# Linear attention with a router gate on one core: one operand split issued a step later, and twelve result stores issued after two more loads

## The chip, the core and the metric

The kernel runs on one core of a Trainium2 chip. The core has five engines that work side by side, each through its own queue in order: TensorE (PE) multiplies matrices, VectorE (DVE), ScalarE (ACT) and GpSimd (POOL) work element by element, and SyncE (SP) issues most of the DMA transfers here. Weight loads of TensorE are shown as a row of their own (PEld); a DMA queue's issuing is shown as SPq. The metric is the time of one execution on the device in microseconds (us), as the median of several runs. A profiled execution is recorded once, and its span is counted from the first to the last recorded event.

## The reference

Four sequences of 512 tokens with 512 features are worked on. All of it is float32.

```python
xn = layernorm(x)                                     # x: (4, 512, 512)
qkv = silu(xn @ w_qkv.T)                              # 16 heads of 128: q, k, v
for each block of 64 tokens, per head:                # kv: running 128x128 state
    o  = (q * q_decay) @ kv + ((q @ k.T) * diag_decay) @ v
    kv = block_decay * kv + (k * k_decay).T @ v
o = norm_w * (o * rsqrt(mean(o * o) + 1e-6))          # mean over all 2048 channels
s = (sigmoid(xn @ w_gate.T) * o) @ w_out.T
scores = softmax(xn @ router_w.T + router_b)          # 64 experts
w8, i8 = top_k(scores, 8)
g = silu(xn * sum(w8) + w8 @ expert_bias[i8])
out = x + s * g
```

## The kernel before, in words

The token blocks of the attention are 128 wide instead of 64 (four chunks, NT = 4, per sequence), which computes the same. The big products keep float32 accuracy with three passes: an operand is split into a high part in a rounded type (split_hi, a copy on ScalarE, L100) and a low part (split_lo, a subtraction on VectorE or GpSimd, L103), and high by high, high by low and low by high are added in PSUM. The projections of two sequences at a time use a scheme with seven products in place of eight (unit, L484).

The work comes in three stages. The first computes v for all sequences and keeps it in DRAM. The second goes through head units: for two pairs of sequences and for each pair of heads one gate unit and two q/k units (L1039 to L1095). A unit issues its seven products, and after each of them the entries of a list, after[0] to after[6], in which other work is placed: the attention of the head before, loads, splits of coming weights. The attention of a head is written in three parts: scores_qk (products sa of k and q, transposes kt of k, the mask product at on VectorE, kd on ScalarE, qd on GpSimd), states (ss, and its running sums st) and attend (o, the product y with gate and norm weight on VectorE, a store of y to DRAM, and a square on ScalarE that GpSimd adds up in sqs). When a q or k comes out of a unit, its silu is done in two parts: the sigmoid is issued at once on ScalarE (L555), and the product on VectorE (L558) is put into a list, deferred, which do_deferred empties later.

The third stage is the output projection, a loop over 64 steps (L1112), one for each sequence and head. A step multiplies the split output weight of its head (wr) with the split y of its head and sequence (yr) into four PSUM banks pos, twelve products in all (o_head, L816). A function, ahead(i, loads, splits) at L1015, issues what the steps need before: loads of y (and of the output weight wo for the first sequence) up to step i + loads, and their splits up to step i + splits. One split step consists of a copy on ScalarE and a subtraction on VectorE for yr, and, for the first sequence, a copy on ScalarE and a subtraction on GpSimd for wr. From step 2 on the pool op2 has four buffers each of yin, woin and yr, so that a load waits until the split of four steps before has read its buffer.

The last head unit issues the first calls of ahead in its lists. After the unit comes do_deferred at L1109, which issues the product of the last k. The attention of the last head is issued in the first three steps of the loop, behind their twelve products each: scores_qk in step 0, states in step 1, attend in step 2 (L1100 to L1104). Its PSUM tiles, those of sa, kt and ss and one of the o, take turns in the three buffers of ps_sc; the products pos are in ps_mm.

After the sixteenth head of a sequence, finish (L808) is called for each of its four token tiles: VectorE scales the bank by the norm and by the gate u (L811), GpSimd (VectorE for the last sequence) adds x (L812), and the result is stored (L813). Behind these come in program order ahead of that step, then the next sequence's first step, which loads wT, the turned routing weights of the next sequence, and the first tile of x (L1149 to L1151). Four steps into a sequence ffn (L764) multiplies wT with the expert biases into pu and begins the next gate u, out of a pool with five buffers; silu_gate (L772) completes it.

All orders on the queues are those of the program text; nothing is reordered by a planner.

## Time and profile before

| | us |
|---|---|
| median of 3 runs | 1069.27 |
| lowest and highest run | 1067.15 and 1069.29 |
| profiled execution | 1068.67 |
| its span | 1066.9 |
| TensorE busy in the span | 1056.2 |
| VectorE, ScalarE, GpSimd busy | 695.6, 476.1, 727.3 |
| last head unit's products end, step 0 of the output projection begins | about 865.7 |
| step 16 (second sequence) begins | about 924.8 |

The mean granted clock of TensorE over the span is 0.997 of full speed. A row of a timeline gives start, length, engine, line, operation, what is written and read, and in brackets how long the engine had been idle and what released it. A row of the chain of work that ended last gives start, length and what the chain was on. Busy TensorE is modelled, since its matmuls are pipelined.

### The profile page before, as it was taken

The page shows a single profiled execution, that of the slowest core. Times are in us where ns is not written, and L with a number is a line of the kernel's source. Part 1 is how long each engine was busy: PE and PEld are TensorE (multiplying, and loading weights), DVE is VectorE, ACT ScalarE, POOL GpSimd, SP SyncE. Part 2 cuts the span into 40 slices and gives each one's busy share as a digit, 9 for nine tenths or more (in the row PEclk, how much of TensorE's full clock was granted, in tenths as well). Part 3 has the DMA queues.
Part 4 walks back from the last instruction along what each step waited for, and adds up shares of the span by engine and source line. Part 5 has one row for each costly group of instructions (what it writes and reads, how often), then busy time and mean ns, then how long its engine had stood idle before and what let it go on. Part 6 is the DMA issues. An engine that isn't in the chain of part 4 may idle for free.

```text
span 1066.9 us, 16491 instructions
## 1 busy us (share of the span) xinstructions
PE 1056.2 (99%) x5771; PEld 910.9 (85%) x5771; DVE 695.6 (65%) x1061; ACT 476.1 (45%) x923; POOL 727.3 (68%) x710
## 2 busy tenths in 40 slices
PE   9999999999999999999999999999999989999998
PEld 8888788888888888888888888888888878888886
DVE  7898876667576666665756756657567556754464
ACT  5555554544444444444444444444444434332321
POOL 5898892868787678777785787777867847612130
PEclk9999999999999999999999999999999999999999
DMA  6557747522423333235722232232222436354351
GB/s 224 184 177 251 262 145 235 160 84 88 136 84 94 103 97 108 75 124 195 254 84 83 87 115 78 85 128 84 84 91 90 149 109 206 119 178 168 98 194 53
DMA packets 109875, 143.11 MB, mean 134 GB/s; under 512 B 9680, under 2 KB 58208, under 8 KB 108896
## 3 DMA queue, kind: packets, MB, share of 16 engines
q1 hardware_dynamic: 108752, 141.35, 40.7%
q8 instruction: 46, 0.75, 0.3%
q10 hardware_dynamic: 1040, 0.71, 0.2%
q14 instruction: 37, 0.30, 0.1%
HBM read 93.24 MB, written 50.87 MB: 135 GB/s over the span
## 4 chain that ended last, share of the span: by engine, by line
PE 93%; DVE 3%; DMA 2%; POOL 1%; SPq 1%; issue 1%; ACT 1%; DVEq 0%; ACTq 0%
PE u_qk L502 28%; PE po L818 16%; PE u_g L502 14%; PE u_v L502 11%; PE sa L675 5%; PE o L712 5%; PE ss L698 4%; PE o L714 4%; PE kt L678 2%; DMA raw_v<-in_w_v_dram 1%; PE lg L318 1%; PE pu L769 1%; DMA v<-vo_v 1%; DVE k L558 1%; POOL ts L268 0%
## 5 line engine op out<-in xcount | busy, mean ns | idle before, releaser
L818 PE MATMUL po<-wr,yr 128*128 128x512 f32 (+1 forms) x777 | 179.5, 389 | 1.0 <-DVE u L811 1.0
L818 PEld LDWEIGHTS po<-wr,yr 128*128 128x128 f32 x777 | 144.5, 188 | 31.2 <-DVE u L811 1.2
L502 PE MATMUL u_qk<-blk_T,ws_qk 128*128 128x512 f32 x576 | 147.1, 395 | 0.0
L724 POOL TENSOR_TENSOR sqs<-sqs,sq 128x512 f32<-128x512 f32 x60 | 78.5, 1309 | 78.3 <-ACT sq L723 78.3
L502 PEld LDWEIGHTS u_qk<-blk_T,ws_qk 128*128 128x128 f32 x576 | 105.7, 188 | 20.5
L103 DVE TENSOR_TENSOR yr<-yin,yr 128x512 fp32r<-128x512 f32 x64 | 71.5, 1127 | 50.1 <-ACT yr L100 50.0
L103 POOL TENSOR_TENSOR ws_qk<-sum_qk,ws_qk 128x512 fp32r<-128x512 f32 x64 | 82.8, 1295 | 30.7 <-ACT ws_qk L100 29.9
L502 PE MATMUL u_qk<-blk_B,wa_qk 128*128 128x512 f32 x384 | 99.1, 393 | 0.0
L558 DVE TENSOR_TENSOR k<-k,sg_k 128x512 f32<-128x512 f32 x64 | 92.3, 1442 | 2.4 <-ACT sg_k L555 2.2
L712 PE MATMUL o<-at,vin 128*128 128x128 f32 x512 | 88.4, 275 | 0.0
L502 PEld LDWEIGHTS u_qk<-blk_B,wa_qk 128*128 128x128 f32 x384 | 70.9, 188 | 14.2
L702 DVE SCALAR_TENSOR_TENSOR st<-st,bdecay,ss 128x128 f32<-128x128 f32 x128 | 41.7, 346 | 61.4 <-ACT st L700 59.1
L555 ACT ACTIVATE sg_k<-k 128x512 f32<-128x512 f32 x64 | 40.5, 632 | 86.6 <-DVE k L493 86.6
L712 PEld LDWEIGHTS o<-at,vin 128*128 128x128 f32 x512 | 74.9, 191 | 2.5
L502 PE MATMUL u_g<-blk_T,ws_g 128*128 128x512 f32 x288 | 76.0, 399 | 0.0
L714 PE MATMUL o<-qd,st 128*128 128x128 f32 x384 | 74.2, 275 | 0.0
L103 POOL TENSOR_TENSOR ws_g<-sum_g,ws_g 128x512 fp32r<-128x512 f32 x32 | 42.7, 1334 | 44.7 <-ACT ws_g L100 44.7
L675 PE MATMUL sa<-q,k 128*128 128x128 f32 x512 | 68.7, 278 | 3.2 <-DVE k L558 3.2
L675 PEld LDWEIGHTS sa<-q,k 128*128 128x128 f32 x512 | 65.1, 193 | 6.6 <-issue 3.2
L777 POOL TENSOR_TENSOR u<-u,sgu 128x512 f32<-128x512 f32 x16 | 20.7, 1292 | 70.1 <-ACT sgu L776 57.4
L716 DVE SCALAR_TENSOR_TENSOR y<-o,nw,gt 128x512 f32<-128x512 f32 x64 | 47.6, 747 | 31.7 <-PE o L714 30.1
L723 ACT ACTIVATE sq<-o 128x512 f32<-128x512 f32 x60 | 35.9, 598 | 71.4 <-POOL sqs L724 43.1
(186 smaller groups left out, 2420.5 us busy)
## 6 DMA issues: line engine op xcount, KB each, us to landing
v<-vo_v SPq DMA_DIRECT2D x64, 256.0 KB, 2.1
raw_qk<-in_w_head_dram SPq DMA_DIRECT2D x64, 256.0 KB, 3.6
vin<-v SPq DMA_DIRECT2D x64, 256.0 KB, 3.6
y<-y SPq DMA_DIRECT2D x64, 256.0 KB, 2.0
yin<-y SPq DMA_DIRECT2D x64, 256.0 KB, 3.0
x<-in_x_dram SPq DMA_DIRECT2D x32, 256.0 KB, 4.3
raw_g<-in_w_head_dram SPq DMA_DIRECT2D x32, 256.0 KB, 3.2
raw_v<-in_w_v_dram SPq DMA_DIRECT2D x16, 256.0 KB, 5.6
```

Of the source, the lines that this page charges most:

```text
L103: eng.tensor_tensor(lo, src, hi.bitcast(F32), ALU.subtract)
L502: nc.tensor.matmul(ps, lhsT, rhs, start=(first and c == 0 and n == 0), stop=(c == KC - 1 and n == len(PASSES) - 1), skip_group_check=not f ...
L555: nc.scalar.activation(sg, src, AF.Sigmoid)
L558: nc.vector.tensor_tensor(dst, src, sg, ALU.mult)
L675: nc.tensor.matmul(pa[:, c], k[:, c], q[:, c], start=True, stop=True)
L698: nc.tensor.matmul(ps[:, c], kd[s][:, c], v_of(b, h, c), start=True, stop=True)
L702: nc.vector.scalar_tensor_tensor(r[:, c], r[:, c - 1], bdecay[:, h : h + 1], ps[:, c], ALU.mult, ALU.add)
L712: nc.tensor.matmul(o, v_of(b, h, c), at[s][:, c], start=True, stop=(c == 0))
L714: nc.tensor.matmul(o, st[s][:, c - 1], qd[s][:, c - 1], start=False, stop=True)
L716: nc.vector.scalar_tensor_tensor(y, po, nw[:, h : h + 1], gts[s], ALU.mult, ALU.mult)
L724: nc.gpsimd.tensor_tensor(sq[b], sq[b], s1, ALU.add)
L818: nc.tensor.matmul(pos[t][:, c], yr[:, yi, bass.ts(t, P)], wos[h][:, wi, c], start=(h == 0 and n == 0), stop=(h in stops and n == len(PASS ...
```

## The change

Two edits are made. The call of ahead in after[6] of the last head unit asks for two split steps in place of three, so that the split of step 2 (h = 2 of the first sequence) is issued by the call of ahead at the top of step 0, behind do_deferred at L1109. The number of loads that the call asks for is the same. In finish the store of a result is put into a list, stores, for the first three sequences; the list is emptied in the next step of the loop, behind its call of ahead. The four stores of each of the three sequences thus stand behind the y loads that are issued by ahead in the last step of the sequence and in the first step of the next. The stores of the last sequence are issued at once as before.

```diff
+    stores = []
+
     def finish(b, t, ps, c=slice(None)):
         u, xt = gates[b, t][:, c], xts[b, t][:, c]
         last = b == B - 1
         nc.vector.scalar_tensor_tensor(u, ps[:, c], rms[b][:, t : t + 1], u, ALU.mult, ALU.mult)
         (nc.vector if last else nc.gpsimd).tensor_tensor(u, u, xt, ALU.add)
-        (nc.scalar if last and t % 2 else nc.sync).dma_start(out=out[tok(b, t), c], in_=u)
+
+        def store():
+            (nc.scalar if last and t % 2 else nc.sync).dma_start(out=out[tok(b, t), c], in_=u)
+        if last:
+            store()
+        else:
+            stores.append(store)
...
             after[3].append(more)
             after[4].append(lambda: ahead(0, 4, 2))
             after[5].append(lambda: load_eb(op))
-            after[6].append(lambda: ahead(0, 6, 3))
+            after[6].append(lambda: ahead(0, 6, 2))
...
         if h < NH - 1:
             ahead(i, 6, 3)
+            while stores:
+                stores.pop(0)()
         if h == 0:
             for t in range(NT):
                 pos[t] = ps_mm.tile([P, F], F32, tag="mm", name=f"po_{b}_{t}")
```

## The prediction

> **What bounds the kernel now.** First the page's busy rows and its chain by line. TensorE is busy 99% of the span and 93% of the chain is its own work, so only its idle time, and the time in which its clock is not full, can be won.

> ```profile
> PE 1056.2 (99%) x5771; PEld 910.9 (85%) x5771; DVE 695.6 (65%) x1061; ACT 476.1 (45%) x923; POOL 727.3 (68%) x710
> PE 93%; DVE 3%; DMA 2%; POOL 1%; SPq 1%; issue 1%; ACT 1%; DVEq 0%; ACTq 0%
> ```

> An average over 1067 us hides a hole, so next the chain in order of time where the change sits, from the end of the last head unit:

> ```profile
> 869.19 0.52 ACT yr L100
> 869.71 0.02 issue
> 869.73 0.04 DVE yr L103
> 869.77 1.25 issue
> 871.01 1.76 DVE k L558
> 872.77 0.14 issue
> 872.91 2.04 PE sa L675 x8
> 874.95 0.64 PE kt L678 x3
> 875.59 3.15 PE po L818 x12
> ```

> VectorE starts the subtraction of the third y split (yr, L103) at 869.73, and only behind it, at 871.01, the product that completes the last k (L558). ScalarE had the sigmoid for that product long before:

> ```profile
> 865.39 0.63 ACT L555 ACTIVATE sg_k<-k 128x512 f32<-128x512 f32 x1 [1.06 <-DVE k L493]
> 872.91 2.04 PE L675 MATMUL sa<-q,k 128*128 128x128 f32 x8 [2.96 <-DVE k L558]
> ```

> The sigmoid ends at 866.02, the last y of the unit (L716) leaves VectorE at 867.21, and VectorE then sits idle 2.52 us in front of a subtraction that waits for ScalarE's copy, while the ready product stands behind it. TensorE idles 2.96 us for that product. Third, the windows of one us (columns: window, length, busy time of PE, PEld, DVE, ACT, POOL, the granted TensorE clock, DMA share, GB/s):

> ```profile
> 871.00:872.00 1.00, 0.00 (x0) 0.00 (x0) 1.00 (x2) 0.00 (x0) 1.00 (x1) 1.00 0.97 344
> 873.00:874.00 1.00, 1.00 (x5) 1.00 (x6) 0.36 (x1) 0.00 (x0) 1.00 (x2) 0.50 0.78 242
> 876.00:877.00 1.00, 1.00 (x6) 0.76 (x5) 0.25 (x1) 1.00 (x3) 0.00 (x0) 0.87 0.00 0
> ...
> 1060.00:1062.00 2.00, 1.03 (x8) 0.83 (x8) 1.93 (x4) 0.00 (x0) 0.00 (x0) 1.00 0.35 131
> 1062.00:1064.00 2.00, 1.01 (x9) 0.80 (x7) 0.98 (x3) 0.00 (x0) 0.00 (x0) 1.00 0.55 197
> ```

> The idle time also costs clock: 0.50 from 873 until a little after 876. From 876 to 1059 TensorE has no gap but two small ones in front of pu, below.

> **Part 1, the third split moved to step 0.** It consists of two ScalarE copies, one VectorE subtraction (yr) and one GpSimd subtraction (wr). No loads move: the call in the last unit still issues loads 4 and 5, and step 0 finds nothing more to load. On ScalarE and GpSimd the neighbours in the queue stay the same, because between the old and the new place only the deferred product is issued, and that is VectorE's. So the edit is one swap on VectorE: product k first, yr subtraction second. Recomputed in order:

> - Product k starts at 867.2. Alone on VectorE this form takes 0.68 us, beside GpSimd up to 1.75 (the four k products of 840 to 880: 1.17 to 1.75). It ends between 867.9 and 868.95, before TensorE is through with the other sequence's sa and kt at 869.95. The second sa, whose PSUM buffer is freed by ScalarE's square at 869.19, follows without a wait and takes 0.9, as the first did at full clock: until 870.85.
> - The yr subtraction keeps its start, 869.73, and its 1.36: until 871.09. The mask product at (L680) of the first sequence is queued behind it, 0.68 more: until about 871.75. This is late next. ps_sc has three buffers, and by their turns the second kt takes the one that this at reads. So TensorE stands from 870.85 to about 871.9 (0.14 of issue, as at 872.77), a new wait of **1.0 us** in place of 2.96.
> - kt 0.33 and the 12 products of step 1, 2.74 (as step 2's at 880.08), at full clock: step 1 ends at 875.0. Before it ended at 878.74. Gain **3.7 us**: 1.96 of idle time, and 1.7 of slow clock and of waking up (2.04 + 0.64 + 3.15 against 0.9 + 0.33 + 2.74 is 1.86, of which 0.14 is lost again in issue).

> [...] Product k would be issued at 867.2, just ahead of GpSimd's square sum at 867.27. [...] The rows show VectorE stretched more often (1.36 for yr beside GpSimd, 0.68 alone), but GpSimd too (wr 1.72 at 870.49 against 1.27). I take the middle, **3.5 us**.

> [...] The nearest rows are the last two windows above: TensorE busy half the time over 4 us, with one gap of 0.97, and the clock stays 1.00. I take no drop. With a drop, some 3.2 us (what it lasted here) at half speed lose 1.6, and the gain is 1.9. Bounds of this part: 1.9, and 4.6 if no gap stays (the second kt in another buffer).

> Does the shift last? yr of step 2 is ready at 871.1 and its wr at 872.2 (unchanged), step 2 would start near 876.4: 4 us of cover. Steps 5 and 6 are tight: GpSimd's wr for step 5 runs 889.21 to 890.96 and TensorE is there at 891.45; step 6 waits 0.3. But these subtractions stand in GpSimd's queue behind the square sums of the last attention (885.93 to 889.25), which follow TensorE's o matmuls, and the loads of that stage stand in SP's queue behind the y stores of the same attention (885.20). All of it moves with TensorE. The loads for steps 4 and 5 are issued at 867.6 to 869.5 and the DMA engines are idle by 875. The shift goes through.

> **Part 2, twelve stores later.** At the end of the first three sequences SP's queue is:

> ```profile
> 911.18 9.89 SPq L785 DMA_DIRECT2D yin<-y  x4
> 926.11 4.98 SPq L813 DMA_DIRECT2D out_dram<-u  x4
> 931.19 0.87 SPq L785 DMA_DIRECT2D yin<-y  x2
> 932.11 0.42 SPq L761 DMA_DIRECT2D wTin<-wTd  x1
> 936.11 0.30 PEld L769 LDWEIGHTS pu<-ebs,wTin 128*128 128x128 f32 x2 [0.37 <-DMA wTin<-wTd]
> ```

> After the change the two y loads stand ahead of the stores. The first (y of step 20) has its buffer at 924.0, the second when the yr subtraction of step 17 ends at 928.2 (first of three from 926.60). The stores that wait behind it catch up at 0.45 each; the last is bound by GpSimd's add at 930.7 either way, and nothing of VectorE, ScalarE or GpSimd waits for a store soon (the pool has five u). The y loads come 3 to 7 us earlier, which hides in slack already there (yr of step 20 is ready at 935.4, wanted at 936.85). What reaches TensorE: wT is issued at 931.15 in place of 932.11, and pu waits 0.37 for it here and 0.28 at 981.60; the third time it does not wait. Pu took 0.68 and 0.60 there against 0.45 elsewhere: gain 0.23 + 0.15, **0.35 us**. Bounds: 0.4 gained, and 0.4 lost if stores and wT collide in the DMA engines.

> **Sum.** 3.5 + 0.35 = 3.85 us. The profiled execution took 1068.67 with a span of 1066.9: it would be 1064.8 with a span of 1063.05. The median of the runs lies 0.6 above it (1069.27), and two of three runs agree on that value, so the forecast is 1069.27 - 3.85 = **1065.4 us**, 0.36% less. About 0.2% (2.1 us, also the spread of the three runs) is what a measurement can tell from no change.

> **Rivals.**
> - The clock drops in the gap that stays. [...] Against: the two windows at the end. Gain 1.9 + 0.35: 1067.0, on the border of what can be told. 10%.
> - The gain is given back in steps 5 to 7, with GpSimd's wr as the bound. For it: the 0.3 wait and GpSimd's unbroken run from 889 to 899. Against: that run starts from TensorE's own attention. Then only part 2 is left: 1068.9. 11%.
> - Slower: the second y load blocks SP. All four stores, wT and the x loads stand behind it, and pu has no slack for wT at two of three boundaries. It decides once wT slips by more than 1.9 us against before at all three: 3 x 1.9 = 5.7 eats 3.5 and adds the 2.1 that can be seen. With 2.3 us of SP issue between the y load and wT, the yr subtraction would have to end at 931.7 and not at 928.2. Then 1071.5 or more. 7%.
> - No gap stays: 4.6 + 0.35, 1064.3. 6%.
> - My forecast: 66%, own range 1064.4 to 1066.3.

> **How the numbers follow.** The forecast and the case without a gap lie on the faster side, 72%, and half of the clock case, 5%; from this I take 3 for the scatter of the runs: 74% faster. Within 0.2% are half of the clock case, the given-back case and that scatter: 19%. Slower 7%. For eight in ten the range goes from 1063.7 (no gap, less scatter) to 1067.8: forecast and clock case are in, the other two rivals out.

> **What would show it.** Right: in the chain near 867, L558 of k ahead of yr L103; no wait of sa for k; a wait of kt of 1 to 1.5 us for at L680; the clock 1.00 in every us from 868 to 878; step 1 ending near 875; pu at about 932.5 and 978 without a wait for wTin; on SP two loads before the four stores. Wrong: 0.5 clock after 872, a wait of po for wr or yr in steps 4 to 7, a longer wait of pu for wTin, or the same wait of sa for k.

## The result, and the profile after

Over ten runs the changed kernel takes 1064.78 us in the median (1063.93 to 1067.52), and the kernel before, over ten runs that now include the three shown above, 1067.78 (1067.10 to 1069.29). The ratio is 0.9967 with a 95% interval of 0.9956 to 0.9978: 3.5 us faster, 2.4 to 4.7 (3.0 by the two medians). The forecast was 3.85 less, 1065.4. The profiled execution took 1063.93 with a span of 1062.2.

The page of the changed kernel, its busy row and chain by engine:

```profile
PE 1053.3 (99%) x5771; PEld 909.4 (86%) x5771; DVE 696.0 (66%) x1061; ACT 476.3 (45%) x923; POOL 728.7 (69%) x710
PE 87%; DVE 1%; issue 0%; ACT 0%; POOL 0%; DVEq 0%; ACTq 0%
```

TensorE's busy time fell by 2.9 us although it does the same matmuls: a matmul at half clock counts at its full length (the eight sa took 2.04 us at a clock of 0.50 in the kernel before, 0.89 at 1.00 in the chain of split_behind below), so slow ones that are gone show here (1.65 of the 2.9, as the interval below shows). The change is best read in the chain of the changed kernel, in order of time (start, length, what):

```profile
868.59 0.52 ACT yr L100
869.10 0.02 issue
869.13 0.04 DVE yr L103
869.16 0.72 issue
869.88 0.02 DVEq L103
869.90 0.51 issue
870.41 0.69 DVE at L680
871.10 0.05 issue
871.15 0.55 PE kt L678 x3
871.70 2.75 PE po L826 x12
```

Product k is gone from the chain; behind the yr subtraction now stands the mask product at, and behind it the second kt. VectorE's rows show where product k went, and the queue of TensorE what is left to wait for (timelines; in brackets the idle time before and its releaser):

```profile
864.38 0.63 ACT L555 ACTIVATE sg_k<-k 128x512 f32<-128x512 f32 x1 [1.07 <-DVE k L493]
866.13 0.68 DVE L558 TENSOR_TENSOR k<-k,sg_k 128x512 f32<-128x512 f32 x1
866.26 1.70 POOL L724 TENSOR_TENSOR sqs<-sqs,sq 128x512 f32<-128x512 f32 x1 [3.12 <-ACT sq L723]
871.15 0.55 PE L678 MATMUL kt<-ident,k 128*128 128x128 f32 x3 [1.32 <-DVE at L680]
```

The last sigmoid of k starts here at 864.38, before at 865.39: this execution came to the edit 1.01 us earlier through stages in which nothing was changed. So all comparisons below are made by one interval, **from the start of that sigmoid to the end of step 1**. It was 878.74 - 865.39 = 13.35 us before and is 874.44 - 864.38 = 10.06 now, 3.29 less. Of these, 1.64 are idle time of TensorE (2.96 before, 1.32 now) and 1.65 its busy time in the interval (10.39 before, 8.74 now), the slow clock that is gone. From there to the end of the span it was 188.16 and is 187.76, 0.40 less. With the 1.01 this makes up the whole difference of the spans, 4.7.

The windows of one us of the changed kernel (columns as above) show TensorE short of work once, and its clock full:

```profile
870.00:871.00 1.00, 0.00 (x0) 0.00 (x0) 1.00 (x2) 0.09 (x1) 1.00 (x1) 1.00 0.88 330
871.00:872.00 1.00, 0.85 (x6) 0.78 (x7) 0.69 (x2) 0.27 (x1) 1.00 (x2) 1.00 0.50 139
873.00:874.00 1.00, 1.00 (x6) 0.84 (x5) 1.00 (x1) 0.34 (x1) 1.00 (x2) 1.00 0.75 234
```

And SP's queue and pu at the second sequence's start (timelines of the changed kernel):

```profile
919.75 4.15 SPq L785 DMA_DIRECT2D yin<-y  x2
923.96 2.81 SPq L817 DMA_DIRECT2D out_dram<-u  x4
926.82 0.45 SPq L761 DMA_DIRECT2D wTin<-wTd  x1
931.68 0.62 PE L769 MATMUL pu<-ebs,wTin 128*128 128x512 f32 x2
```

The y loads are ahead of the stores, the four stores go out in 2.81 us in place of 4.98, and wT is issued 4.86 us ahead of pu, where it was 4.0.

### The profile page after: what moved, and what is told of

Its sections match the earlier page's. It is cut to its first block, busy times and chain, and to the rows that moved or that the text cites. A ratio compares the mean times of both kernels' runs of the same rounds, so it can differ in the third digit from the quotient of the medians.

```text
span 1062.2 us, 16490 instructions
## 1 busy us (share of the span) xinstructions
PE 1053.3 (99%) x5771; PEld 909.4 (86%) x5771; DVE 696.0 (66%) x1061; ACT 476.3 (45%) x923; POOL 728.7 (69%) x710
## 4 chain that ended last, share of the span: by engine, by line
PE 87%; DVE 1%; issue 0%; ACT 0%; POOL 0%; DVEq 0%; ACTq 0%
PE u_qk L502 28%; PE po L826 16%; PE u_g L502 14%; PE u_v L502 7%; PE o L712 5%; PE sa L675 5%; PE ss L698 4%; PE o L714 4%; PE kt L678 2%; PE pu L769 1%; DVE k L558 0%; PE ssq L741 0%; PE pw L388 0%; DVE u L813 0%; POOL sqs L724 0%
## 5 line engine op out<-in xcount | busy, mean ns | idle before, releaser
L103 POOL TENSOR_TENSOR ws_qk<-sum_qk,ws_qk 128x512 fp32r<-128x512 f32 x64 | 82.8, 1295 | 30.4 <-ACT ws_qk L100 29.5
L103 DVE TENSOR_TENSOR yr<-yin,yr 128x512 fp32r<-128x512 f32 x64 | 71.7, 1135 | 39.5 <-ACT yr L100 39.1
L558 DVE TENSOR_TENSOR k<-k,sg_k 128x512 f32<-128x512 f32 x64 | 91.3, 1427 | 2.4 <-ACT sg_k L555 2.2
L555 ACT ACTIVATE sg_k<-k 128x512 f32<-128x512 f32 x64 | 40.5, 632 | 86.7 <-DVE k L493 86.7
L103 POOL TENSOR_TENSOR ws_g<-sum_g,ws_g 128x512 fp32r<-128x512 f32 x32 | 42.7, 1336 | 44.8 <-ACT ws_g L100 44.8
L716 DVE SCALAR_TENSOR_TENSOR y<-o,nw,gt 128x512 f32<-128x512 f32 x64 | 47.6, 747 | 31.6 <-PE o L714 30.1
L675 PE MATMUL sa<-q,k 128*128 128x128 f32 x512 | 67.7, 275 | 0.2 <-DVE k L558 0.2
L675 PEld LDWEIGHTS sa<-q,k 128*128 128x128 f32 x512 | 64.3, 191 | 3.5 <-DVE q L558 0.6
```

What stands on the lines that cost most here:

```text
L103: eng.tensor_tensor(lo, src, hi.bitcast(F32), ALU.subtract)
L555: nc.scalar.activation(sg, src, AF.Sigmoid)
L558: nc.vector.tensor_tensor(dst, src, sg, ALU.mult)
L675: nc.tensor.matmul(pa[:, c], k[:, c], q[:, c], start=True, stop=True)
L716: nc.vector.scalar_tensor_tensor(y, po, nw[:, h : h + 1], gts[s], ALU.mult, ALU.mult)
```

## The experiments

Theory A is that of the prediction: two instructions change places on VectorE, which takes TensorE's wait for the last k away and with it the slow clock that followed; the stores give a few tenths.

**The two parts apart.** split_only has this line alone:

```diff
-            after[6].append(lambda: ahead(0, 6, 3))
+            after[6].append(lambda: ahead(0, 6, 2))
```

> Only the third split is moved; the stores stay where they were. Theory A (the gain is the swap of two instructions on VectorE, which takes away TensorE's wait for the last k and the slow clock behind it): from the start of the last k sigmoid to the end of step 1 it was 13.35 us in the kernel before and 10.06 in the changed one; here again 10.0 to 10.1, and the whole time 3.3 us less than before, ratio 0.9969. Theory B (most of the gain is scatter of the stages ahead of the edit, or the stores): 13.3 us in that interval, or a time within 1 us of before. pu still waits for wT at the second and third sequence's start.

Measured: 1064.4 us, ratio 0.9964 (0.9952 to 0.9977). stores_only is the other part, with ahead(0, 6, 3) back in the last unit:

> Only the stores are moved; the third split stays in the last head unit. Theory A: the wait of sa for k (about 3 us) and the clock of 0.50 are back, 13.35 us from the last k sigmoid to the end of step 1, and pu takes 0.45 us at all three sequence starts: 0.4 us less than before, ratio 0.9996, not to be told from no change. Theory B (the stores carry the gain): 2 us less or more.

Measured: 1067.37 us, ratio 0.9994 (0.9987 to 1.0001). Its timeline of TensorE has the old wait, and two of its windows the low clock; the line of split_only has the new wait:

```profile
872.29 1.29 PE L675 MATMUL sa<-q,k 128*128 128x128 f32 x8 [2.95 <-DVE k L558]
872.40:872.80 0.40, 0.40 (x4) 0.40 (x5) 0.35 (x1) 0.00 (x0) 0.40 (x1) 1.00 0.70 236
873.20:873.60 0.40, 0.40 (x5) 0.40 (x4) 0.00 (x0) 0.00 (x0) 0.40 (x1) 0.50 0.85 256
```

```profile
871.35 0.55 PE L678 MATMUL kt<-ident,k 128*128 128x128 f32 x3 [1.31 <-DVE at L680]
```

The interval is 874.65 - 864.59 = 10.06 us in split_only and 878.10 - 864.78 = 13.32 in stores_only. The gain is the split's. The stores' part is too small for the runs to separate from nothing, and the traces leave its size open. In stores_only pu waits at none of the three starts, and from the end of step 1 to the end of the span it takes 187.80 us against 188.16 before. But split_only, with the stores in their old place, takes 187.85: there pu waits only 0.18 us, at the fourth sequence's start, where waits at the second and third were expected. Over all kept traces pu waits at six of nine starts with the stores in the old place and at four of 33 with them moved, so the order seems to help, but the 0.4 of this one pair of profiles is not shown to be its worth.

In stores_only the clock falls some 0.8 us after sa has begun (at 872.29), in the kernel before as it begins: in these two traces the drop does not come at one distance from the first matmul after the gap.

**What the kt waits for.** In kt_own_buffer the second kt of step 0 gets a PSUM buffer outside ps_sc, as the head units do it:

```diff
-        [lambda: scores_qk(b1, hl, attp), lambda: scores_qk(b0, hl, attp)],
+        [lambda: scores_qk(b1, hl, attp), lambda: scores_qk(b0, hl, attp, (ps_o, "o"))],
```

> The changed kernel with the second kt of step 0 in the buffer of ps_o, as in all other units, in place of its turn in ps_sc. If the wait of kt for at (1.32 us) comes from the turn of the three buffers, it goes: 8.7 to 8.8 us from the last k sigmoid to the end of step 1 against 10.06, and 1.3 us less than the changed kernel in all (3.5 + 1.3 = 4.8 less than before, ratio 0.9955). If the kt waits for something else (k, the earlier kd), the interval stays at 10.06.

In split_behind the buffers stay, and the third split is issued behind the scores of step 0, so that at stands ahead of yr on VectorE:

```diff
-            ahead(i, 6, 3)
+            ahead(i, 6, 2 if i == 0 else 3)
...
             for f in last_steps[i]:
                 f()
+            if i == 0:
+                ahead(0, 6, 3)
```

> The changed kernel with the third split issued behind the scores of step 0, so that both mask products at stand ahead of the yr subtraction on VectorE, while the PSUM turns stay as they are. If the wait of kt is for at queued behind yr, it shrinks from 1.32 us to under 0.2, and step 1 ends 8.5 to 8.8 us after the last k sigmoid (kt_own_buffer: 8.52), the whole being 1.3 us less than the changed kernel, ratio to before 0.9955. The rival: yr and wr of step 2 now come late, since both kd stand ahead of their copies on ScalarE and both qd ahead of wr on GpSimd; then step 2 waits for wr by up to 1 us and the gain over the changed kernel is under 0.5 us.

The chain of kt_own_buffer, and under it that of split_behind:

```profile
869.23 0.89 PE sa L675 x8
870.12 0.33 PE kt L678 x3
870.45 2.75 PE po L826 x12
```

```profile
871.93 0.89 PE sa L675 x8
872.82 0.33 PE kt L678 x3
873.15 2.75 PE po L826 x12
```

Both run from sa into kt without a gap. The interval is 873.20 - 864.68 = 8.52 us and 875.89 - 867.37 = 8.52. The times: 1063.08 with a ratio to before of 0.9954 (0.9939 to 0.9970), and 1063.11 with 0.9962 (0.9949 to 0.9976). So the wait that stayed needed both, the shared buffer and the order on VectorE; either cure takes it whole. The rival of split_behind, a late wr of step 2, did not show: step 2 follows ss without a wait. The last pair of runs put both cures into one kernel, beside the changed kernel on the same chip:

> The changed kernel once more, to stand beside the next one on the same chip: ratio to before 0.9967 as in the first measurement (0.9956 to 0.9978), mean granted clock 0.999 or above in every run, where most runs of before have 0.996 to 0.998.

> The changed kernel with both cures of the wait that stayed: the second kt in the buffer of ps_o, and the third split behind the scores of step 0. Either cure alone brought 8.52 us from the last k sigmoid to the end of step 1 against 10.06. By theory A nothing of the wait is left for the second to take: 8.5 us again, ratio to before 0.9953, 1.5 us under the changed kernel. If the cures take different waits, the interval goes below 8.4 us.

The changed kernel measured 1064.48 us, 0.9960 (0.9944 to 0.9976), interval 10.05 us. With both cures it was 1062.91, 0.9947 (0.9932 to 0.9962), interval 872.75 - 864.23 = 8.52: nothing is left for the second cure, and this version is ahead of the changed kernel by the 1.5 us of the interval. The medians, 1.57 apart, agree with it, though with six runs each the two ratios' intervals overlap.

**Is the slow clock a cost of its own?** fill12 gives TensorE something to do while it waits for k, in the kernel before:

```diff
+    FILL = 12
+
+    def fill(n):
+        ps = ps_o.tile([P, P], F32, tag="o", name="fill")
+        for _ in range(n):
+            nc.tensor.matmul(ps, ident, ident, start=True, stop=True)
...
-        [lambda: scores_qk(b1, hl, attp), lambda: scores_qk(b0, hl, attp)],
+        [lambda: scores_qk(b1, hl, attp), lambda: fill(FILL), lambda: scores_qk(b0, hl, attp)],
```

> The kernel before, with twelve matmuls of the identity put between the first kt and the second sa of step 0, where TensorE waits 2.96 us for k; some 2.7 us of added work whose result nobody reads. Theory A, with the clock as a part of its own: sa still starts when k is done (7.5 us after the last k sigmoid's start), but at full clock, so step 1 ends 11.5 us after the sigmoid in place of 13.35, and the kernel is 1.8 us faster than before although work was added, ratio 0.9983. Theory C (the slow clock has another cause than the idle time): clock 0.50 stays, 13.35 us or more, no gain.

The timeline of TensorE in fill12 (each of the twelve matmuls stands as two rows), and two of its windows:

```profile
871.32 2.84 PE L1103 MATMUL fill<-ident 128*128 128x128 f32 x24
874.45 1.13 PE L675 MATMUL sa<-q,k 128*128 128x128 f32 x8 [0.29 <-DVE k L558]
873.00:874.00 1.00, 1.00 (x11) 0.97 (x9) 1.00 (x1) 0.00 (x0) 1.00 (x2) 1.00 0.66 207
876.00:877.00 1.00, 1.00 (x6) 0.82 (x5) 0.31 (x1) 1.00 (x3) 0.12 (x1) 1.00 0.17 66
```

Locally it went as expected: k comes at the same distance, the clock stays 1.00, and the interval is 878.68 - 866.92 = 11.76 us in place of 13.35. The whole time did not follow: 1068.06 us, ratio 1.0002 (0.9992 to 1.0012), where 0.9983 was expected. In its profile wT loads were late at the sequence starts (1.8 us of weight loads waiting for them), so the same was tried on top of stores_only:

> The kernel with only the stores moved, and the twelve matmuls of the identity of fill12 in it, so that late wT loads can't hide what the clock is worth. Theory A (idle time of TensorE costs twice, as waiting and as a slow clock afterwards): 11.5 to 11.8 us from the last k sigmoid to the end of step 1 against 13.32 in stores_only, pu without a wait, and the whole 1.5 us less than stores_only: ratio to before 0.9979 against 0.9994. Theory C (clock without weight in the whole time, some other queue sets the end): ratio as stores_only, 0.9994, or above.

Again the interval shrank (878.87 - 867.12 = 11.75, against 13.32) and the time did not: 1067.51 us, 0.9998 (0.9986 to 1.0010). In its profile one wT transfer took 6 us to land, and the pu behind it waited, although wT was issued 6.1 us ahead of it:

```profile
931.28 6.03 DMA wTin<-wTd
937.31 0.04 issue
937.35 0.73 PE pu L769 x2
```

Part of the miss has a reading in the runs themselves. Of 70 runs of the kernel before that were taken beside the experiments, 57 have a mean granted clock of 0.998 or less, and 13 have 0.999 or more. The 13 have a median of 1066.79 us, the 57 one of 1068.19. In stores_only it is 7 runs at 1065.96 against 15 at 1067.73. All 44 runs of the five kernels without the long wait have 0.999 or more. So runs with the slow clock take 1.4 to 1.8 us longer, which fits the 1.59 us that fill12 takes off the interval, but not every execution has it: a filler can only save it in those that do, which leaves some 1.3 (57 of 70 times 1.59) of the 1.8 us expected.

The two profiles show where their gain went. From the end of step 1 to the end of the span fill12 takes 189.12 us and fill12_stores 189.13, against 188.16 in the kernel before and 187.80 in stores_only: 0.96 and 1.33 us are given back, where pu waits for wT. Whether the other runs of the fill kernels lose it in the same way, and whether the filler has a part in the late wT, stays open, since one execution of each was recorded.

**How long a gap does it take?** Two kernels were to lengthen the wait of kt by issuing the at of the sequence that comes first in step 0 more than once, at_1_more with this edit and at_3_more with 3 + 1 in place of 1 + 1:

```diff
-        nc.vector.tensor_tensor(
-            at[s], pa, d[:, 0, None, :].to_broadcast([P, NT, P]), ALU.mult
-        )
+        for _ in range(1 + 1 if s == (B - 1, NH - 1) else 1):
+            nc.vector.tensor_tensor(
+                at[s], pa, d[:, 0, None, :].to_broadcast([P, NT, P]), ALU.mult
+            )
```

> The changed kernel with the first mask product of the last head issued twice (the same result), 0.6 us more on VectorE ahead of kt: kt waits 1.9 us. If the clock falls only with a gap near 3 us, it stays 1.00 and step 1 ends 10.7 us after the last k sigmoid (10.06 + 0.6). If a gap of 2 us is enough, the clock goes to 0.50 for about 3 us and it is 12 us or more.

> The same with three more mask products, 1.8 us on VectorE: kt waits 3.1 us. By theory A the clock falls to 0.50 as in the kernel before, and step 1 ends 13.4 us or more after the last k sigmoid (10.06 + 1.8 + 1.5). If the clock in the kernel before fell for another reason than the idle time, it stays 1.00 and the interval is 11.9 us.

Both missed what they were made for. One execution of each gave an interval of 874.33 - 865.24 = 9.09 and 873.86 - 864.80 = 9.06 us, shorter than the changed kernel's. The line of at_1_more tells why:

```profile
871.01 0.55 PE L678 MATMUL kt<-ident,k 128*128 128x128 f32 x3 [0.32 <-ACT kd L685]
```

The second kt is in another of the three buffers now, that of the first kt, which kd on ScalarE frees. Which buffer a tile gets is thus not a plain turn of three: it changed with the number of instructions on another engine. Next the yr subtraction of step 2 was repeated instead, twice in yr_x2 and, with 3 in place of 2, three times in yr_x3:

```diff
-        split_lo(nc.vector, yr[:, 1], y, yr[:, 0])
+        for _ in range(2 if (b, h) == (0, 2) else 1):
+            split_lo(nc.vector, yr[:, 1], y, yr[:, 0])
```

> The changed kernel with the yr subtraction of step 2 issued twice (the same result), nothing else touched, in place of the repeated mask products, which moved kt to another PSUM buffer. By theory A kt still waits for at, and at stands behind both subtractions: the second one takes 0.7 to 1.8 us (GpSimd's wr runs beside it until 872), so kt waits 2.0 to 3.1 us and step 1 ends 10.8 to 11.9 us after the last k sigmoid if the clock stays 1.00; 1 to 1.7 us more if it falls to 0.50. If kt waits for another thing than the VectorE queue, it stays at 10.06.

> The same with three subtractions: kt waits 2.7 to 4.5 us. By theory A the clock falls to 0.50 as in the kernel before, and step 1 ends 13 us or more after the last k sigmoid. If the clock stays 1.00 beyond a gap of 3 us, the idle time alone is not what lowered it in the kernel before.

yr_x2 kept the buffer, and its kt waits as long as sa did in the kernel before:

```profile
876.01 0.55 PE L678 MATMUL kt<-ident,k 128*128 128x128 f32 x3 [2.98 <-DVE at L680]
```

With 2.98 us idle the clock stayed at 1.00, and the interval was 879.32 - 867.57 = 11.75 us, the value expected without a drop: at starts 7.70 us after the sigmoid in place of 6.03, 1.67 later, and step 1 ends 1.69 later. yr_x3 moved the kt to the other buffer again (it waits 0.32 for kd) and tells nothing about a longer gap; there it is ss that waits for at, 0.8 us.

The clock records of the traces set the gaps near 3 us apart. In all 14 kept traces every stretch at full clock lasts a whole number of times 3.413 us (254 times in the kernel before up to the drop, 309 times in the changed kernel), and the low clock behind the gap in the kernel before and in stores_only lasts 3.41 us, once. So in these traces the clock changes only at the ends of stretches of that length, called windows here. These are such windows, cut at those ends (columns as above; the second column is their length, the third how long TensorE was busy), first of the kernel before, around its gap and around its last work, then of yr_x2, then of the changed kernel:

```profile
869.44:872.85 3.41, 0.50 (x5) 0.27 (x3) 3.12 (x3) 1.26 (x3) 3.41 (x3) 1.00 0.94 305
872.85:876.27 3.42, 3.36 (x14) 3.20 (x15) 1.20 (x2) 0.64 (x2) 1.72 (x2) 0.50 0.38 125
...
1060.59:1064.00 3.41, 1.45 (x10) 1.13 (x9) 2.36 (x5) 0.00 (x0) 0.00 (x0) 1.00 0.37 134
1064.00:1066.90 2.90, 0.00 (x0) 0.00 (x0) 0.00 (x0) 0.00 (x0) 0.00 (x0) 0.50 0.14 45
```

```profile
871.04:874.45 3.41, 1.98 (x18) 1.79 (x17) 2.10 (x2) 2.11 (x4) 2.70 (x3) 1.00 0.88 300
874.45:877.87 3.42, 1.86 (x10) 1.60 (x11) 2.25 (x4) 1.28 (x3) 2.73 (x3) 1.00 0.43 129
877.87:881.28 3.41, 3.41 (x23) 3.03 (x22) 1.45 (x4) 1.18 (x4) 1.28 (x1) 1.00 0.40 123
```

```profile
868.60:872.02 3.42, 2.10 (x18) 1.83 (x16) 2.56 (x3) 1.78 (x4) 3.36 (x3) 1.00 0.84 282
```

In the kernel before the gap lies in one window but for its last 0.06 us, which leaves TensorE 0.50 us of work there, and the next window has half the clock. In stores_only the window has 0.83 us of work, and the clock falls behind it too. In yr_x2 the end of a window at 874.45 cuts the gap in two, both windows keep 1.86 us or more, and the clock stays. Over all windows at full clock of the 14 traces the clock fell behind each one with 1.58 us of work or less (the 1.58 at the end of the kernel with both cures, 1.33 at the end of the changed kernel) and behind none with 1.86 or more. In these traces it is thus the idle time within one window that sorts them, and by an estimate from the two nearest windows the limit lies between 1.55 and 1.83 us (3.41 less 1.86 and less 1.58). By that estimate a gap of 1.32 us alone stays below it wherever it falls. A gap of 2.96 passes it unless the end of a window cuts it near its middle; if all positions were equally likely, that is by estimate 4 to 21% of executions (twice the limit less 2.96, over 3.41), and 13 of 70 runs, 19%, have the high clock.

## Why the prediction was right, point by point

- **The bound and the wait.** Right. The old order comes back with its wait in stores_only and goes in split_only.
- **The swap.** Product k starts where it was put, 1.75 us after the sigmoid's start (1.81 predicted), and ScalarE's and GpSimd's orders stayed. The new wait was 1.32 us (1.0 to 1.5 predicted), of kt for at.
- **The size of part 1.** The 3.5 us that the sum takes is a choice of mine which no run shows; the recomputed rows gave 3.7, and the trace has 3.29. The 0.4 between 3.7 and 3.29 is seen on GpSimd's side: product k, issued 0.13 ahead of GpSimd's sum, took 0.68, and the sum 1.70 in place of 1.29. ScalarE's next square waited for that sum, the yr copy stood behind the square, and the yr subtraction began 4.75 after the sigmoid in place of 4.34. Before, the order was the other way round: k was issued at 871.01 behind GpSimd's wr (870.49, 1.72 long, until 872.21) and ended 0.56 after it, at 872.77. The rows with VectorE stretched, 1.75 for k and 1.36 for yr, are both of a VectorE instruction issued behind a GpSimd one (yr at 869.73, GpSimd's sum at 869.27), which product k after the swap is not.
- **The clock.** No drop in the gap that stayed, as forecast, but the reason given for it was wrong, and that it held was luck. The two windows at the end of the kernel before, from 1060 to 1064, were read as a case of TensorE half idle at full clock. The clock fell right behind them, at 1064.00: the window that ended there had 1.45 us of work, by the lines above. The gap of 1.32 us left 2.1 us of work in its window, more than the 1.86 of yr_x2, where the clock stayed too. The sum also took the drop of the kernel before as certain. A mean clock of 0.998 or less, taken here as its sign, is in 57 of 70 runs, so the gain over many runs is some 0.3 us smaller than over two profiles of which the first had it (a fifth of 1.6).
- **The PSUM buffer.** That at holds the buffer which kt wants is shown by kt_own_buffer. "By their turns" was too simple as a reason: at_1_more and yr_x3 got another buffer without a change of order.
- **The shift goes through.** Right: the weight loads of po wait 0.3 for wr and 0.3 for yr after step 1, as before, and from the end of step 1 to the end nothing was given back: the time there fell by 0.40.
- **The stores.** The way is as described: the four stores catch up, the last one is bound by GpSimd's add, and wT goes out 0.98 us earlier, counted from the first of GpSimd's adds (6.35 against 7.33). The size, 0.35 predicted, is not shown. This pair of profiles has 0.40, but split_only, without the moved stores, is only 0.09 behind the changed kernel over the same stretch (187.85 against 187.76). The cover of pu is thin all the same, as the 6 us transfer in fill12_stores shows.
- **The absolute time.** Two of three runs agreeing on 1069.27 was taken as a sign for that value. Ten runs put the median at 1067.78. The level was thus 1.5 too high and the gain 0.85 above the difference of the two medians (3.00), which partly cancel in 1065.4 against 1064.78. That the forecast came so near is in this part luck.

Of the rivals, none came: no drop, nothing given back, SP not blocked. That no gap stays is what the two cures made of it, 8.52 us.

## What to carry to other kernels

When work is issued ahead of time, look at what stands ready behind it in an in-order queue: the split here waited 2.5 us for its own input with a finished product behind it that TensorE needed. After such a swap ask at once what is second in the queue now; here it was one more small product and a PSUM buffer, worth another 1.5 us. Read a local edit by an interval between two events near it, since the stages ahead scatter by as much as such an edit is worth (the last k sigmoid starts between 864.23 and 867.57 in these profiles).

## What was not expected of the hardware

In these rows a product on VectorE and a GpSimd instruction beside it did not both keep their length. The shortest product k of the kernel before takes 0.68 us. The two issued at 871.01 and 863.52, behind a GpSimd instruction that then ran 1.20 and 0.62 us more, took 1.76 and 1.17 and ended 0.56 and 0.55 after it. In the other order, in the changed kernel, the product issued 0.13 us ahead of GpSimd's sum took 0.68, and the sum 1.70, 0.41 more than before. What the two engines hold each other up on is not shown by these runs.
